# Spreading projections and softmax halves evenly over the slots of two attentions in a fused four-layer kernel

## The chip, the cores and the metric

The kernel runs as one program on one core of one Trainium2 chip. The core has five instruction streams that run beside each other: TensorE (PE in the profile; its weight loads are the row PEld), VectorE (DVE), ScalarE (ACT), GpSimd (POOL), and SyncE (SP), which in this kernel mostly issues transfers. Each stream executes strictly in its own order and waits on semaphores for the others. The metric is device time in microseconds (us) of one execution. Before the change the median of three runs was 3443.88 us (3443.7 to 3446.11).

## The reference, cut to what matters

Four layers are applied in turn to `x` of shape (8, 256, 512), all in fp32: an attention over features (layer 0), an RWKV block with a sequential scan (layer 1), a transformer decoder layer (layer 2) and a bilinear block with batch norm (layer 3). The change lies in the two attentions of layer 2, a self attention and a cross attention with the same arithmetic, eight batches each:

```python
def attention(q, k, v, mask):                      # 16 heads of 32, 256 queries, 256 keys
    scores = einsum('bhqd,bhkd->bhqk', q, k) / sqrt(HD)
    scores = scores * mask - 10000.0 * (1.0 - mask)
    probs = softmax(scores, axis=-1)
    return einsum('bhqk,bhkd->bhqd', probs, v)

ln_out = layernorm(hidden_states, ln1_s, ln1_b)
q, k, v = split(ln_out @ w_qkv + b_qkv, 3)
x = hidden_states + merge_heads(attention(...)) @ w_ao + b_ao       # then the same with w_q, w_kv, w_co,
                                                                    # keys and values from encoder_states
```

## The kernel before

The class `Middle` computes layer 1 and the two attentions. Its method `loop` has two parts. The first is the scan of layer 1, 64 steps ("slots" 0 to 63). The second is the attention part, again 64 slots, numbered on from `A0 = 64`. One *run* is one attention of one batch: runs 0 to 7 (`a_`) are the self attentions, 8 to 15 (`c_`) the cross attentions. A run has four slots (`CT = 4`), one for each group of four heads (`ct`); a slot has two halves `h2` of two heads each.

For each slot these functions exist (line numbers of the kernel before):

- `scores` (L1119): 8 products of PE, into four PSUM banks, one for each head.
- `masked` (L1131, L1134), a half: DVE multiplies the scores by the mask, adds the mask's offset, writes them to SBUF as `pe` and takes the maximum.
- `exps` (L1143), a half: ACT exponentiates in place and sums.
- `divided` (L1151, L1153), a half: DVE takes the reciprocal of the sums, POOL multiplies `pe` by it.
- `turn` (L1163, L1167, L1169), a half: DVE transposes 32x32 blocks of `pe` into `dt`, SP writes `dt` to a DRAM tile in one transfer, and four gathers from DRAM bring it back as `pt`, with keys on the partitions.
- `values` (L1182, L1186): 8 products of PE of `pt` with the values, then ACT takes the result out of PSUM as `cx`.

Everything else of a run is put as *fillers* at a position relative to the run's first slot, a table of positions that `fill.until` works off: the fetch of the batch (`at_fetch`), its layer norm (`at_norm`, `at_normed`, `at_norm_T`), encoder states and mask (`at_inputs`), halves of the projections (`at_q`, `at_k` by feature pairs at L817; `at_v`, `at_out` by row halves at L881), the residual (`at_residual`, L1079, L1081, L1087) and the store (`at_store`, L1093). A second table of the same positions says when the weights of the four projections are needed and until when, and from it the weight loads are placed.

Three things set the order on the engines. PE runs in exactly the order in which the code calls it (a manual schedule). Instructions wrapped in `pin` keep the program's order on their engine. All the rest on DVE, ACT and POOL, and SP's transfers, are placed by a scheduler between these.

In the loop before, the scores and masks stand two slots ahead of the block transposes, and the exponentials and divisions one slot ahead. Within a slot `n` the order is: exponentials of `n+1`, both transposes of `n`, scores of `n+2`, then in turn for both halves the masks of `n+2` and the divisions of `n+1`, then fillers up to position `n+0.5`, the values of `n-1`, and the rest of the fillers. In each run the fillers put projection halves into its slots unevenly: the positions modulo four give one half (`q`) in the first slot, four (two of `k`, two of `out`) in the second, one (`v`) in the third and two (`q`, `v`) in the fourth. PSUM has eight banks of one tag (`mm`), handed out in turn to scores, projections, transposed norms and values. `pt` has two buffers for each half, `pe` six.

Fillers of the last batches of layer 1 (the channel mix, at positions up to `A0 + 24`) still run beside the first runs of the attention part, and the first runs' own norm and projections run beside the last slots of the scan.

Of the kernel before, what the change touches and what calls it, by code (L numbers as in the profile page):

```python
# [17 lines left out]
B, S, D = 8, 256, 512  # L18
# [603 lines left out]
class Middle:  # L622
# [62 lines left out]
    def plan(self):  # L685
        g, cp, wpool = self.g, self.cp, self.wpool
        nc, I = g.nc, g.I
# [25 lines left out]
        def mm(name):  # L713
            return ps.tile([P, 2, S], F32, tag="mm", name=name, bufs=bufs[0])
# [180 lines left out]
        def spread(b, ct, hf):  # L895

            v_ = t_["v", b]
            vb = vbs[b, ct, hf] = ps.tile([P, NG, 2, S], F32, tag="vb", name="vb", bufs=1)
            for j in range(2):
                for n in range(NG):  # L900
                    r = slice(32 * n, 32 * n + 32)
                    nc.tensor.matmul(  # L902
                        vb[:, n, j, 1:S], lhsT=esel[r, 2 * hf + j, :], rhs=v_[r, ct, 0 : S - 1],
                        start=True, stop=True,
                    )
# [99 lines left out]
        pin = lambda ins: self.tc.keep_in_program_order(ins)  # L1005
# [89 lines left out]
        def at_load(W, src, col):  # L1095
            t_[W, 0] = rows_of(g.weight(wpool, I[src], col, W))
# [17 lines left out]
        def scores(i, ct):  # L1114
            sps = t_["sp", i, ct] = [mm("sp") for _ in range(NH)]
            for qt in range(ST):
                for h in range(NH):
                    r = slice(h * HD, (h + 1) * HD)
                    nc.tensor.matmul(  # L1119
                        sps[h][:, qt, :], lhsT=t_["aq", i][r, ct, qt * P : (qt + 1) * P],  # L1120
                        rhs=t_["ak", i][r, ct, :], start=True, stop=True,
                    )

        def masked(i, ct, h2):


            pe = t_["pe", i, ct, h2] = wk.tile([P, 2 * ST, S], F32, tag="a", name="pe", bufs=6)
            nmax = t_["nmax", i, ct, h2] = sm.tile([P, 2 * ST], F32, tag="nmax", name="nmax", bufs=4)
            for h in range(2):
                sp = t_["sp", i, ct][2 * h2 + h]  # L1130
                pin(nc.vector.scalar_tensor_tensor(sp, sp, 1.0 / HD ** 0.5, t_["mk", i], ALU.mult, ALU.mult))  # L1131
                for qt in range(ST):
                    r = ST * h + qt
                    pin(nc.vector.tensor_tensor_reduce(  # L1134
                        pe[:, r, :], sp[:, qt, :], t_["mb", i][:, qt, :], -1.0, 3.0e38, ALU.add, ALU.min,
                        nmax[:, r : r + 1],
                    ))

        def exps(i, ct, h2):
            pe, nmax = t_["pe", i, ct, h2], t_.pop(("nmax", i, ct, h2))  # L1140
            ssum = t_["ssum", i, ct, h2] = sm.tile([P, 2 * ST], F32, tag="ssum", name="ssum", bufs=4)
            for r in range(2 * ST):
                nc.scalar.activation(  # L1143
                    pe[:, r, :], pe[:, r, :], AF.Exp, bias=nmax[:, r : r + 1], scale=-1.0,
                    accum_out=ssum[:, r : r + 1],
                )

        def divided(i, ct, h2):
            pe = t_["pe", i, ct, h2]
            rinv = sm.tile([P, 2 * ST], F32, tag="rinv", name="rinv", bufs=4)  # L1150
            pin(nc.vector.reciprocal(rinv, t_.pop(("ssum", i, ct, h2))))  # L1151
            for r in range(2 * ST):
                pin(nc.gpsimd.tensor_scalar(  # L1153
                    pe[:, r, :], pe[:, r, :], rinv[:, r : r + 1], 1.0, ALU.mult, ALU.mult
                ))

        def turn(i, ct, h2):


            pe = t_.pop(("pe", i, ct, h2))  # L1160
            dt = wk.tile([P, 4, S], F32, tag="xn", name="dt", bufs=6)
            pt = t_["pt", i, ct, h2] = wk.tile([P, 4, S], F32, tag=("r", "w4")[h2], name="pt")
            pin(nc.vector.transpose(  # L1163
                dt.rearrange("p c (x q) -> p x c q", q=32), pe.rearrange("p x (k c q) -> p (x k) c q", k=ST, c=4)
            ))
            to = g.dram([4, 32, 4, S], f"pt{i}_{ct}_{h2}")
            nc.sync.dma_start(out=to.rearrange("r k c f -> (r k) c f"), in_=dt)  # L1167
            for c in range(4):
                nc.sync.dma_start(out=pt[32 * c : 32 * c + 32], in_=to[:, :, c].rearrange("r k f -> k r f"))  # L1169
# [48 lines left out]
        fill = self.fill = Filler()  # L1218
# [4 lines left out]
        A0 = 8 * B  # L1223
        for i in range(len(runs)):
            for at, fn, *args in (
                (-7.1, at_fetch), (-5.95, at_inputs), (-6.6, at_norm), (-5.9, at_normed), (-5.3, at_norm_T),
                (-4.8, at_q, 0), (-3.8, at_q, 1), (-2.8, at_k, 0), (-2.3, at_k, 1), (-1.3, at_v, 0), (-0.8, at_v, 1),
                (3.9, at_residual), (5.2, at_out, 0), (5.6, at_out, 1), (6.3, at_store),
            ):
                fill.put(A0 + CT * i + at, lambda i=i, fn=fn, args=args: fn(i, *args))  # L1230
        runs.append(("m_", 0))
# [14 lines left out]
        for pre, i, q, kv, o in (("a_", 0, "w_qkv", "w_qkv", "w_ao"), ("c_", B, "w_q", "w_kv", "w_co")):  # L1246
            c = D if q == kv else 0
            for W, lo, hi, src, col in (
                ("wq", -4.8, -3.8, q, 0), ("wk", -2.8, -2.3, kv, c), ("wv", -1.3, -0.8, kv, c + D), ("wo", 5.2, 5.6, o, 0)
            ):  # L1250
                lo, hi = A0 + CT * i + lo, A0 + CT * (i + B - 1) + hi
                spans.append((lo, hi, lambda W=pre + W, src=src, col=col: at_load(W, src, col)))
# [3 lines left out]
        for lo, hi, fn in spans:  # L1256
            free.sort()
            at = free.pop(0)
# [4 lines left out]
        def loop(psums):  # L1263
            every = [(b, ct, hf) for b in range(B) for ct in range(CT) for hf in range(2)]
            bufs[0] = 3
            fill.until(-0.001)
            spread(*every[0])
            for n, at in enumerate(every):
                states(*at)
                fill.until(n + 0.95)  # L1270
                if n:
                    gather(*every[n - 1])
                fill.until(n + 0.99)
                if n + 1 < len(every):
                    spread(*every[n + 1])
            gather(*every[-1])

            psums.close()
            self.ps = psums.enter_context(self.tc.tile_pool(name="atp", bufs=8, space=PSUM))
            bufs[0] = 8  # L1280
            every = [(i, ct) for i in range(2 * B) for ct in range(CT)]
            for at in every[:2]:
                scores(*at)
                masked(*at, 0)
                masked(*at, 1)
            for h2 in range(2):
                exps(*every[0], h2)
                divided(*every[0], h2)
            fill.until(A0 + 0.5)
            for n, at in enumerate(every):  # L1290
                one, two = every[n + 1 : n + 2], every[n + 2 : n + 3]
                for nxt in one:
                    exps(*nxt, 0)
                    exps(*nxt, 1)
                turn(*at, 0)
                turn(*at, 1)
                for nxt in two:
                    scores(*nxt)
                for h2 in range(2):
                    for nxt in two:  # L1300
                        masked(*nxt, h2)
                    for nxt in one:
                        divided(*nxt, h2)
                fill.until(A0 + n + 0.5)
                if n:
                    values(*every[n - 1])
                fill.until(A0 + n + 0.99)
            values(*every[-1])
            fill.until(999)
            psums.close()  # L1310
            return t_["ln", 2 * B]
# [454 lines left out]
```

## Time and profile before

| what | value |
|---|---|
| median of 3 runs | 3443.88 us |
| the profiled execution | 3449.99 us, its span 3448.2 us |
| attention part in it | from the first scores, 2170.66 us, to the first product of the next stage, 2949.84 us |
| PE busy over the span | 3211.6 us (93%) |
| DVE, ACT, POOL busy | 2409.5 us (70%), 1604.9 us (47%), 1667.2 us (48%) |
| transfers by SP's queue | 523.60 MB, 48.4% of the 16 engines' span |

A group of instructions is shown as line, engine, operation, written and read tiles, count, then busy time and mean duration, then idle time before it and who ended that. In a timeline the first column is the start in us from the span's start, the second the duration, the last brackets the idle time of the engine before it and what released it. SPq rows are the issues of transfers on SP. A table by windows gives, for each stretch, busy time of PE, weight loads, DVE, ACT and POOL with instruction counts in brackets, then the granted clock of PE (1.00 is full), the busy share of the DMA engines and GB/s.

### The profile page before, as it was taken

Reading aid. Unit: us, or ns where it says so; the run is one execution under the profiler, and the core shown is the slowest. Engines: PE = TensorE matmul, PEld = TensorE weight load, DVE = VectorE, ACT = ScalarE, POOL = GpSimd, SP = SyncE. Lnnn points to the kernel's source line nnn. Section 1 sums busy time; section 2 is a strip of 40 time slices with the busy share of each in tenths; the row PEclk is TensorE's granted clock in tenths of the full one; section 3 lists DMA queues with packets and bytes.
Section 4 is the critical chain, followed back from the end, with each engine's and each line's share of the span. In section 5 each row is a group of like instructions: output and inputs, shape, how many; then the busy total and the mean of one; then the engine's idle time right before and its main releaser. Section 6 shows DMA issues by size and latency. Waiting matters only on the chain. (4 is left out here: it accounts for less than half of the span.)

```text
span 3448.2 us, 68784 instructions
## 1 busy us (share of the span) xinstructions
PE 3211.6 (93%) x26496; PEld 2282.7 (66%) x26496; DVE 2409.5 (70%) x4175; ACT 1604.9 (47%) x4000; POOL 1667.2 (48%) x1776
## 2 busy tenths in 40 slices
PE   9999999999999988889999998899899996899999
PEld 6677777777777765555666665555555553689996
DVE  5667666666666663888788787767777776677771
ACT  4455555555555554233433334566656664323223
POOL 7533333333333222556566665344444443688872
PEclk9999999999999998989999999899999998899999
DMA  8666665665756533212232332578787877500002
GB/s 281 224 195 198 187 198 173 203 198 183 222 175 211 180 100 117 86 50 90 95 104 92 117 96 97 154 233 237 230 246 236 242 240 218 175 1 1 1 13 86
DMA packets 277366, 533.09 MB, mean 155 GB/s; under 512 B 25056, under 2 KB 153712, under 8 KB 272944
## 3 DMA queue, kind: packets, MB, share of 16 engines
q1 hardware_dynamic: 274144, 523.60, 48.4%
q8 instruction: 211, 3.46, 0.4%
q10 hardware_dynamic: 2224, 3.28, 0.3%
q0 software_dynamic: 672, 1.81, 0.2%
q14 instruction: 115, 0.94, 0.1%
HBM read 411.15 MB, written 117.44 MB: 153 GB/s over the span
## 5 line engine op out<-in xcount | busy, mean ns | idle before, releaser
L391 POOL TENSOR_SCALAR pe<-pe,rinv 128x512 f32<-128x512 f32 x256 | 177.8, 695 | 613.7 <-DVE rinv L390 611.1
L368 DVE TENSOR_REDUCE nmax<-sp 128x2 f32<-128x1024 f32 x256 | 309.0, 1217 | 182.6 <-PE sp L363 182.6
L933 POOL TENSOR_TENSOR rs<-a,r 128x1024 f32<-128x1024 f32 x128 | 303.3, 2386 | 242.4 <-DVE a L928 211.6
L1153 POOL TENSOR_SCALAR pe<-pe,rinv 128x256 f32<-128x256 f32 x512 | 236.3, 481 | 342.1 <-DVE rinv L1151 319.4
L377 ACT ACTIVATE pe<-sp,nmax 128x512 f32<-128x512 f32 x512 | 347.5, 683 | 11.2 <-ACT nmax L373 0.2
L1143 ACT ACTIVATE pe<-pe,nmax 128x256 f32<-128x256 f32 x512 | 255.9, 502 | 207.8 <-DVE nmax L1134 203.1
L403 DVE STREAM_TRANSPOSE pt<-pe 128x1024 f32<-128x1024 f32 x256 | 312.8, 1232 | 24.2 <-POOL pe L391 15.4
L432 PE MATMUL av<-pt,vr 32*64 32x256 f32 x8192 | 266.0, 390 | 41.2 <-issue 32.8
L928 DVE TENSOR_TENSOR_SCAN a<-w,vb 128x1024 f32<-128x1024 f32 x128 | 287.2, 2276 | 5.0
L432 PEld LDWEIGHTS av<-pt,vr 32*64 32x64 f32 x8192 | 209.3, 136 | 110.0 <-issue 65.8
L363 PE MATMUL sp<-k,q 64*64 64x512 f32 x2048 | 266.3, 612 | 5.6 <-ACT pe L377 5.6
L373 ACT ACTIVATE nmax<-nmax 128x2 f32<-128x2 f32 x256 | 52.0, 203 | 398.6 <-DVE nmax L368 398.5
L1163 DVE STREAM_TRANSPOSE dt<-pe 128x1024 f32<-128x1024 f32 x128 | 156.9, 1234 | 69.7 <-POOL pe L1153 68.6
L303 PEld LDWEIGHTS gp<-t,ws 128*128 128x128 f32 x1512 | 184.8, 192 | 30.7 <-ACT pe L396 11.4
L303 PE MATMUL gp<-t,ws 128*128 128x128 f32 x1512 | 202.1, 277 | 2.2 <-POOL ws L289 1.4
L396 ACT ACTIVATE pe<-pe,rinv 128x512 f32<-128x512 f32 x256 | 182.7, 730 | 41.2 <-DVE rinv L390 41.2
L924 DVE TENSOR_TENSOR vb<-vb,k 128x1020 f32<-128x1020 f32 x128 | 157.2, 1228 | 4.4
L1182 PE MATMUL cp<-pt,av 128*32 128x256 f32 x1024 | 93.4, 422 | 69.3 <-DMA pt<-pt 57.1
L1445 ACT ACTIVATE h<-h,pvec 128x256 f32<-128x256 f32 x124 | 55.9, 502 | 199.9 <-DVE h L1414 162.7
L902 PE MATMUL vb<-v,mconstc 32*128 32x255 f32 x1024 | 98.8, 441 | 52.6 <-DVE a L928 52.6
L390 DVE RECIPROCAL rinv<-ssum 128x2 f32<-128x2 f32 x256 | 41.2, 161 | 147.3 <-ACT pe L377 147.3
L455 PEld LDWEIGHTS op<-av_sb,wo 128*128 128x128 f32 x512 | 93.3, 192 | 55.9 <-issue 27.5
(310 smaller groups left out, 7618.8 us busy)
## 6 DMA issues: line engine op xcount, KB each, us to landing
pt<-dt SPq DMA_DIRECT2D x128, 512.0 KB, 4.3
pt<-pt SPq DMA_DIRECT2D x512, 128.0 KB, 3.9
ws<-sqk SPq DMA_DIRECT2D x110, 512.0 KB, 4.9
wqk<-in_wqk_dram SPq DMA_DIRECT2D x70, 512.0 KB, 5.5
vr<-v SPq DMA_DIRECT2D x128, 256.0 KB, 4.6
ws<-sv SPq DMA_DIRECT2D x56, 512.0 KB, 4.8
wv<-in_wv_dram SPq DMA_DIRECT2D x36, 512.0 KB, 5.3
v<-vT SPq DMA_DIRECT2D x64, 256.0 KB, 2.6
```

The costliest lines, as they stand in the source:

```text
L303: nc.tensor.matmul(out[:, hf * P : (hf + 1) * P], lhsT=w[n](hf, k), rhs=a[n](hf, k), start=k == 0, stop=k == ST - 1,)
L363: nc.tensor.matmul(sp[a * 64 : (a + 1) * 64, h, :], lhsT=qs[b, 2 * un + a][r, ic], rhs=ks[b, 2 * un + a][r, :], start=True, stop=True,)
L368: nc.vector.tensor_reduce(nmax, sp, AX.X, ALU.max, negate=True)
L377: nc.scalar.activation(pe[:, h, :], sp[:, h, :], AF.Exp, bias=nmax[:, h : h + 1], scale=1.0 / DH ** 0.5, accum_out=ssum[:, h : h + 1],)
L391: nc.gpsimd.tensor_scalar(pe[:, 0, :], pe[:, 0, :], rinv[:, 0:1], 1.0, ALU.mult, ALU.mult)
L396: nc.scalar.mul(pe[:, 1, :], pe[:, 1, :], rinv[:, 1:2])
L403: nc.vector.transpose(pts[b, un][:, it], pe)
L432: nc.tensor.matmul(av[r][h * DH : (h + 1) * DH], lhsT=vr[rows_, kb, h * DH : (h + 1) * DH], rhs=pt[rows_, :, h, 32 * kb : 32 * kb + 32], s ...
L928: nc.vector.tensor_tensor_scan(a.rearrange("p n l -> p (n l)"), w4.rearrange("p n l -> p (n l)"), vb[:, 4 * n2 : 4 * n2 + 4, :].rearrange( ...
L933: nc.gpsimd.tensor_tensor(rs, a, rb, ALU.mult)
L1143: nc.scalar.activation(pe[:, r, :], pe[:, r, :], AF.Exp, bias=nmax[:, r : r + 1], scale=-1.0, accum_out=ssum[:, r : r + 1],)
L1153: pin(nc.gpsimd.tensor_scalar(pe[:, r, :], pe[:, r, :], rinv[:, r : r + 1], 1.0, ALU.mult, ALU.mult))
```

## The change

Three edits. First, the loop of the attention part is written anew as a stream of half slots: in slot `n` the scores of `n+1` come first; then twice, for each half `k` of slot `n+1`: masks of `k`, exponentials of `k`, division of `k-1`, transpose of `k-2`; then all the slot's fillers; then the values of `n-1`, last in the slot. Scores and masks are now one slot ahead instead of two, and there is one slot of prologue instead of two. Second, the fillers' positions change so that each slot of a run has two projection halves: both of `v` (with the transposed norm of the next run between them) in the first, `q` and `out` in the second, `k` and `out` in the third, `q` and `k` in the fourth; fetch, norm, inputs and weight loads move with them, and they stand one to two slots later. Third, the exponentials are pinned in program order on ACT.

```diff
@@ exps
             for r in range(2 * ST):
-                nc.scalar.activation(
+                pin(nc.scalar.activation(
                     pe[:, r, :], pe[:, r, :], AF.Exp, bias=nmax[:, r : r + 1], scale=-1.0,
                     accum_out=ssum[:, r : r + 1],
-                )
+                ))
@@ plan: fillers of a run
-                (-7.1, at_fetch), (-5.95, at_inputs), (-6.6, at_norm), (-5.9, at_normed), (-5.3, at_norm_T),
-                (-4.8, at_q, 0), (-3.8, at_q, 1), (-2.8, at_k, 0), (-2.3, at_k, 1), (-1.3, at_v, 0), (-0.8, at_v, 1),
-                (3.9, at_residual), (5.2, at_out, 0), (5.6, at_out, 1), (6.3, at_store),
+                (-5.2, at_fetch), (-4.6, at_norm), (-4.1, at_normed), (-3.5, at_norm_T), (-3.1, at_inputs),
+                (-2.8, at_q, 0), (-1.8, at_k, 0), (-0.8, at_q, 1), (-0.3, at_k, 1), (0.2, at_v, 0), (0.7, at_v, 1),
+                (4.1, at_residual), (5.7, at_out, 0), (6.7, at_out, 1), (6.8, at_store),
@@ plan: use of the weights
-                ("wq", -4.8, -3.8, q, 0), ("wk", -2.8, -2.3, kv, c), ("wv", -1.3, -0.8, kv, c + D), ("wo", 5.2, 5.6, o, 0)
+                ("wq", -2.8, -0.8, q, 0), ("wk", -1.8, -0.3, kv, c), ("wv", 0.2, 0.7, kv, c + D), ("wo", 5.7, 6.7, o, 0)
@@ loop
-            for at in every[:2]:
-                scores(*at)
-                masked(*at, 0)
-                masked(*at, 1)
-            for h2 in range(2):
-                exps(*every[0], h2)
-                divided(*every[0], h2)
-            fill.until(A0 + 0.5)
-            for n, at in enumerate(every):
-                one, two = every[n + 1 : n + 2], every[n + 2 : n + 3]
-                for nxt in one:
-                    exps(*nxt, 0)
-                    exps(*nxt, 1)
-                turn(*at, 0)
-                turn(*at, 1)
-                for nxt in two:
-                    scores(*nxt)
-                for h2 in range(2):
-                    for nxt in two:
-                        masked(*nxt, h2)
-                    for nxt in one:
-                        divided(*nxt, h2)
-                fill.until(A0 + n + 0.5)
-                if n:
+            stream = [(i, ct, h2) for i, ct in every for h2 in range(2)]
+            for n in range(-1, len(every)):
+                if n + 1 < len(every):
+                    scores(*every[n + 1])
+                for k in (2 * n + 2, 2 * n + 3):
+                    if k < len(stream):
+                        masked(*stream[k])
+                        exps(*stream[k])
+                    if 0 < k <= len(stream):
+                        divided(*stream[k - 1])
+                    if 1 < k:
+                        turn(*stream[k - 2])
+                fill.until(A0 + n + 0.95)
+                if n > 0:
                     values(*every[n - 1])
                 fill.until(A0 + n + 0.99)
             values(*every[-1])
```

## The prediction

> **What bounds the kernel now.** I read first the table by windows over the attention part, cut at the first scores, at the point where the channel mix has mostly run out, at the last scores but two, and at the next stage's first product.
>
> ```profile
> 2171.00:2411.80 240.80, 229.81 (x1215) 138.57 (x1207) 175.52 (x516) 146.67 (x448) 97.95 (x175) 0.97 0.75 219
> 2411.80:2879.80 468.00, 423.13 (x2361) 252.02 (x2361) 356.85 (x1050) 280.11 (x874) 194.83 (x374) 0.93 0.79 238
> 2879.80:2949.80 70.00, 41.84 (x193) 17.16 (x192) 31.43 (x87) 19.96 (x65) 21.54 (x40) 0.73 0.81 240
> ```
>
> In the first stretch PE (first figure after the length) is busy 95%, and from 2200 on 98%: nothing but less work would shorten it. In the second, 468 us, PE is busy 90% at a clock of 0.93, DVE 76%: neither is full. The third, the drain, has PE busy 60% at 0.73.
>
> Next the timeline of PE over one run of the second stretch, for its work and its holes.
>
> ```profile
> 2646.63 1.15 PE L1119 MATMUL sp<-ak,aq 32*128 32x256 f32 x16
> 2647.71 1.07 PE L1182 MATMUL cp<-pt,av 128*32 128x256 f32 x16
> 2648.71 3.70 PE L881 MATMUL projs<-c_wv,enc 128*128 128x512 f32 x8
> 2652.24 1.04 PE L83 MATMUL ln_tp<-ident,axn 128*128 128x128 f32 x8
> ...
> 2673.95 3.70 PE L881 MATMUL projs<-c_wo,cx 128*128 128x512 f32 x8
> 2677.49 3.62 PE L817 MATMUL proj<-enc,c_wk 128*128 128x256 f32 x16
> 2681.03 1.07 PE L1182 MATMUL cp<-pt,av 128*32 128x256 f32 x16
> 2682.03 3.70 PE L881 MATMUL projs<-c_wo,cx 128*128 128x512 f32 x8
> 2685.57 3.62 PE L817 MATMUL proj<-enc,c_wk 128*128 128x256 f32 x16
> 2689.12 1.15 PE L1119 MATMUL sp<-ak,aq 32*128 32x256 f32 x16
> ...
> 2712.48 0.63 PE L1182 MATMUL cp<-pt,av 128*32 128x256 f32 x4 [2.28 <-DVE nmax L1134]
> 2714.61 1.92 PE L1182 MATMUL cp<-pt,av 128*32 128x256 f32 x12 [1.51 <-DMA pt<-pt]
> 2716.47 2.09 PE L1119 MATMUL sp<-ak,aq 32*128 32x256 f32 x16
> ```
>
> From start to start: scores 1.08, values 1.00, a projection half 3.54, transposed norm 0.97. A run's PE work at full clock is 4x1.08 + 4x1.00 + 8x3.54 + 0.97 = 37.6 us. But scores of the same place in the run stand at 2411.78 and 2869.39, ten runs apart: 45.8 us a run. Two things show where 8 us go. Between the scores at 2672.88 and 2689.12 lie four projection halves, 16.2 us, in which DVE has only 8 to 9 us of work; in the lighter slots PE in turn waits, 2.28 and 1.51 us here. And after these waits PE is slow: the same scores take 2.09 instead of 1.15 us.
>
> Then the timeline of SP, for the way from a transpose to the values, and of DVE, for half a slot.
>
> ```profile
> 2890.10 0.32 SPq L1167 DMA_DIRECT2D pt<-dt  x1
> 2890.53 4.34 SPq L1169 DMA_DIRECT2D pt<-pt  x8
> ```
>
> ```profile
> 2703.41 0.68 DVE L1131 SCALAR_TENSOR_TENSOR sp<-sp,mk 128x512 f32<-128x512 f32 x1
> 2706.24 0.17 DVE L1151 RECIPROCAL rinv<-ssum 128x4 f32<-128x4 f32 x1
> 2708.39 1.25 DVE L1163 STREAM_TRANSPOSE dt<-pe 128x1024 f32<-128x1024 f32 x1 [0.85 <-POOL pe L1153]
> ```
>
> On SP a single write of `dt` is followed by eight gathers, the last four of which need it. Half a slot of masks takes DVE 2.83 us (2703.41 to 2706.24), the reciprocal 0.08, a transpose 1.17 net. The transpose waits for POOL, 44.5 us in the second stretch.
>
> **The change part by part.**
>
> *Projections, two to a slot.* No instruction is added or removed: 64 slots keep their 8+8 products, 16 masks and maxima, eight exponentials, 2 transposes, 10 transfers. PE's slots become 10.1 us (two `v` and the norm) and three times 9.2 (1.08 + 2x3.54 + 1.00). DVE's slot is 2x(2.83 + 0.08 + 1.17) = 8.2, plus a run's two residual adds, two statistics, two aggregations and one small product at 0.67, 0.67, 0.17 and 0.16: 3.2 a run, so 9.0 a slot. ACT: eight times 0.69, 0.47 for `cx`, about 1 of drains: 7.0, and once a run 3.1 of tables and layer norm. All are under 10. The 16.2 us hole of DVE is gone.
>
> *Half slots in turn.* A division of half k-1 is issued after the masks of k, its transpose after the masks of k+1, 4.1 us later; POOL needs 1.85 for four of its multiplications. So the transpose's waits for POOL go, except where the residual's two adds (2.5 us) fall between. An exponential's half ends 4.0 us after its masks began, and the reciprocal comes at 7.0: 3 us spare, which covers table loads and drains. These cost nothing while that spare lasts; beyond it DVE waits. Pinning fixes the same order and costs nothing by itself.
>
> *Values at the slot's end.* This adds the new wait. On PE behind the values stand the scores of the next slot but one half-step of DVE away: if `pt` is late, PE, then DVE, then ACT and POOL wait. The loop goes over two slots: scores start to first mask 1.2 us (2170.66 to 2171.85), DVE's slot 9.0, issue 0.1, write landed, four gathers issued, landed, values 1.0. For a write issued alone: the eight gathers at 2890.53 took 4.34 us against 3.66 for eight without a wait, so the fifth left about 2.9 us after its write at 2890.10. Ahead of it on SP now stand the write's own issue, mostly one other transfer (0.5 to 1.0) and the four gathers of the first half (4x0.46): 2.8 to 3.3. I take 3.1. To the last gather's issue 3x0.46 = 1.4, landing 4.0 (median of 168). Together 1.2 + 9.0 + 0.1 + 3.1 + 1.4 + 4.0 + 1.0 = 19.8 us for two slots. The DMA engines are 0.79 busy at 45.8 us a run; at 42 that is 0.86. The part of a landing above its minimum (4.0 less 2.6) I stretch by half for this, 0.7 on each of the two transfers: 21.2 us. So a run lasts 42.4 us, above PE's 37.6. The bounds: 38.5 if the loop hides (PE's work and 0.9 of entries), and 50.4 if the way stays as in the old pair of halves, where it took 14.0 us from the transpose's end at 2700.58 to the values at 2714.61 (loop 25.2). I take the value near the lower one because that old row holds a second write, a blocked encoder load ahead of it and eight gathers behind, and the single write at 2890.10 is the new pattern. Gain: 10 runs x (45.8 - 42.4) = 34 us.
>
> *Clock.* At 2.28 + 1.51 us of waits the scores that follow run at half speed. The forecast leaves about 1.2 us of wait in a slot, in one piece, which I expect to stay warm: the run from 2646.63 to 2689.12 had waits up to 1.97 and ran warm, in 42.5 us.
>
> The Trainium skill, "TensorE: Matmul & The Clock Gate", section "Part 1: The HAM clock gate", says that PE falls to half clock after an idle window of about 3.4 us and needs as long a busy one to recover. It speaks against a wait in every slot; the row above agrees that it is the clock, but falls after two waits of 2.28 and 1.51 with work between. By that rule alone nothing is lost at my 1.2 us, and by the row's pattern a run in which that happens costs 3 us (45.7 against 42.5 for the warm run).
>
> *Start.* Before the first scores PE's order loses both `v` of run 0 and one `q` and a norm of run 1: 3x3.54 + 1 = 11.6 us that move from the scan, where DVE is the bound, into a stretch where PE is. Against that, PE idled 7.9 us in 2170 to 2200 in the two-slot prologue, now filled, and the scan's end has DVE waits of 5.7 and 3.8 behind such fillers. Between +11.6 and -9; I take 0, the sum's middle.
>
> *Drain.* From scores of slot 60 (2869.39) to 2949.84 it took 80.5 us, since SP held three writes in order (gathers 4 us late), and the late transposes stood behind a pinned residual add that waited 7.46 us for PE. Now: slots with `q`+`k`, `v`+`v` and one `out`, 3x10.6; then 9.0 of DVE, 3.5 for the last division and transpose, 10 to `pt`, 1.9 of values and 8 of `out` at the low clock: 64. Gain 16 (8 to 18).
>
> *SP, POOL, weights.* Encoder loads stood ahead of writes and waited for `v` (34.7 us in 240); now they come after the slot's second write, when `v` is done. Their cover is gone if PE lags DVE by over 1 us. POOL's other work (norm, mask offset, residual: 1.5, 0.6, 2.5 us a run) fits in its idle half. The next stage's first weights are issued among the last gathers instead of after them (eight at 2934.59); PE did not wait for them, I count nothing. PSUM: the next scores need banks whose masks ended 1 to 2 us earlier: nothing, below 2 us of lag.
>
> **The sum.** 3449.99 - 34 - 16 - 0 = 3400.0 for an execution like the profiled one, which is 6.1 above the median: 3394.
>
> **The rivals.**
> 1. *PE becomes the bound.* The loop stays under 19 us. For it: writes alone land at 2.6 at best, the first stretch shows PE at 98%. Against: DMA busy 0.86. Runs of 38.5: -73, drain -18: 3353.
> 2. *No gain in the runs.* The way from transpose to `pt` is 12.5 us, loop 22.9, run 45.8; the drain alone remains: 3428.
> 3. *Slower.* The same way keeps the old 14.0 us: landings of 7.4 (the longest seen) at the busier queue. For it: scores stood two slots ahead before and hid this; now they don't. Run 50.4, +46 over ten; drain -8: 3482. It decides against the old kernel from a way of 13.3 us on, where 10 runs cost the drain's 16.
>
> **How the numbers follow.** Forecast 0.52 (own range 3372 to 3420), rival 1 0.18, rival 2 0.10, rival 3 0.20. A measurement of this kernel tells about 0.2% (7 us) from no change. Rival 2 gives the chance of no change (half of its spread) 0.05; faster 0.75, slower 0.20. Range: 3350 to 3452 leaves out rival 3.
>
> **What would show it.** Right: in the middle stretch scores 10 to 11 us apart, clock 0.97 or more, waits of values for `pt` of 1 to 2 us in most slots, no waits of transposes for POOL, drain near 64 us. Wrong: values waiting over 3 us with scores at 2.1 us (rival 3), PE without holes (rival 1), reciprocals waiting for ACT (the spare of 3 us used up).

## The result, and the profile after

The changed kernel takes 3456.23 us (median of 5 runs, 3455.25 to 3463.92) against 3443.88 for the kernel before (5 runs): a ratio of 1.0046, 95% interval 1.0028 to 1.0064. It is slower by 0.46%, where 3394 us was forecast. The profiled execution took 3462.03 us, its span 3460.3.

The table by windows of the changed kernel, cut as before at the first scores, at the scores of slots 20 and 60, and at the next stage's first product (busy time of PE, weight loads, DVE, ACT and POOL, then clock, DMA share, GB/s):

```profile
2168.00:2410.90 242.90, 230.86 (x1236) 139.59 (x1236) 176.40 (x518) 151.89 (x454) 103.41 (x183) 0.98 0.76 222
2410.90:2885.50 474.60, 412.22 (x2322) 247.34 (x2320) 346.74 (x1032) 278.08 (x860) 191.81 (x370) 0.94 0.80 231
2885.50:2961.30 75.80, 50.23 (x252) 24.56 (x251) 37.81 (x104) 24.90 (x81) 19.40 (x39) 0.80 0.85 243
```

The start is neutral. The middle stretch holds ten runs (scores of slot 20 to scores of slot 60): 474.6 us, where 457.6 stood before and 424 was forecast. The drain, the third line, is 75.3 from start to start, before 80.5, forecast 64. The profiled execution missed the forecast of 3400.0 for one execution by 62.0 us; this splits into -0.9 at the start, 50.6 in the ten runs, 11.3 in the drain and 1.0 behind it.

The timeline of PE of the changed kernel, first a stall, then a run from scores to scores without a long one:

```profile
2590.77 0.62 PE L1182 MATMUL cp<-pt,av 128*32 128x256 f32 x4
2600.37 1.92 PE L1182 MATMUL cp<-pt,av 128*32 128x256 f32 x12 [8.98 <-DMA pt<-pt]
2602.22 2.09 PE L1119 MATMUL sp<-ak,aq 32*128 32x256 f32 x16
...
2694.25 1.15 PE L1119 MATMUL sp<-ak,aq 32*128 32x256 f32 x16
...
2715.82 1.15 PE L1119 MATMUL sp<-ak,aq 32*128 32x256 f32 x16
...
2736.88 1.37 PE L1119 MATMUL sp<-ak,aq 32*128 32x256 f32 x16
```

From 2694.25 to 2736.88 a run takes 42.6 us, the forecast's length; two of the ten take 43.0 or less, the others 45 to 58. In the first rows the values wait 8.98 us for `pt`; the scores behind them run at half speed (2.09). A second such wait of 9.62 us stands at 2793.44. On SP the reason for the first of them reads as follows:

```profile
2583.39 1.74 SPq L1169 DMA_DIRECT2D pt<-pt  x4
2585.98 6.09 SPq L1167 DMA_DIRECT2D pt<-dt  x2
2594.56 0.38 SPq L1021 DMA_DIRECT2D mk<-in_mask_b_dram  x1
2595.06 3.98 SPq L1169 DMA_DIRECT2D pt<-pt  x8
```

The row of two writes, 6.09 us from the first's start to the second's end, holds the second half of one slot and the first half of the next; the four gathers that the values wait for are issued behind both and behind a mask's load, as the first four of the eight at 2595.06.

Last, what DVE and PE waited for in the ten runs (us in total, times, longest), in the kernel before and then in the changed one:

```profile
DVE dt L1163 <- POOL pe L1153: 44.5, 34, 6.4
DVE sp L1131 <- PE sp L1119: 17.2, 12, 1.9
PE cp L1182 <- DMA pt<-pt: 28.2, 16, 3.5
```

```profile
DVE sp L1131 <- PE sp L1119: 85.5, 29, 7.7
DVE away L1032 <- ACT ln_rstd L61: 16.9, 10, 3.4
DVE dt L1163 <- POOL pe L1153: 11.5, 3, 4.1
DVE ln_stats L58 <- DMA axi<-xa: 7.7, 3, 4.3
PE cp L1182 <- DMA pt<-pt: 56.0, 27, 9.6
```

The transposes' waits for POOL fell as forecast, from 44.5 to 11.5 us. In their place DVE waits 85.5 us for scores (before 17.2) and PE 56.0 for `pt` (before 28.2): DVE has become dependent on PE, which stands at the values. The statistics of the layer norm now wait for the fetch, which they did not in the kernel before.

### The profile page after: what moved, and what is told of

Read it like the earlier page. It is cut to its first block, busy times and chain, and to the rows that moved or that the text cites. A ratio compares the mean times of both kernels' runs of the same rounds, so it can differ in the third digit from the quotient of the medians.

```text
span 3460.3 us, 68721 instructions
## 1 busy us (share of the span) xinstructions
PE 3202.3 (93%) x26496; PEld 2286.0 (66%) x26496; DVE 2406.2 (70%) x4175; ACT 1607.7 (46%) x4000; POOL 1663.7 (48%) x1776
## 5 line engine op out<-in xcount | busy, mean ns | idle before, releaser
L377 ACT ACTIVATE pe<-sp,nmax 128x512 f32<-128x512 f32 x512 | 347.0, 683 | 11.2
L1182 PE MATMUL cp<-pt,av 128*32 128x256 f32 x1024 | 103.4, 424 | 94.4 <-DMA pt<-pt 83.0
L1182 PEld LDWEIGHTS cp<-pt,av 128*32 128x32 f32 x1024 | 36.8, 115 | 167.2 <-issue 104.9
```

Of the source, the lines that this page charges most:

```text
L377: nc.scalar.activation(pe[:, h, :], sp[:, h, :], AF.Exp, bias=nmax[:, h : h + 1], scale=1.0 / DH ** 0.5, accum_out=ssum[:, h : h + 1],)
```

## The experiments

All times are medians beside runs of the kernel before on the same chip; "a run" is a tenth of the ten runs from slot 20 to 60, measured at DVE's first mask product of a slot, in one profile; clock and DMA share are those of that stretch, where they were read. The profiled execution can lie off the median: that of x5_oldplaces took 14 us more, x1_order's 8 more, z5_closed_stats's 7 less. "Tied" means that SP's transfers stand in the order of x1_order, described below; x4_all and all runs whose names begin with x7, y or z1 to z5 are tied too.

| label | loop | places of projections | ratio to before, 95% | us | a run | clock, DMA |
|---|---|---|---|---|---|---|
| before | old | old | 1 | 3439 to 3444 | 46.0 | 0.93, 0.79 |
| after | new | even | 1.0046 (1.0028 to 1.0064) | 3456.2 | 47.5 | 0.94, 0.80 |
| x5_oldplaces | new | old | 1.0141 (1.0123 to 1.0159) | 3491.0 | 49.8 | 0.92, 0.76 |
| x6_evenold | old, tied | even, one slot earlier | 0.9920 (0.9905 to 0.9935) | 3416.5 | 43.4 | 0.96, 0.85 |
| x1_order | new, tied | even | 1.0043 (1.0026 to 1.0060) | 3454.2 | 46.7 | 0.94, 0.81 |
| x2_mask | new | even | 1.0064 (1.0041 to 1.0086) | 3464.1 | 47.1 | |
| x3_norm | new | even | 0.9996 (0.9984 to 1.0008) | 3440.7 | 44.7 | 0.98, 0.84 |
| x4_all | new | even | 0.9990 (0.9977 to 1.0004) | 3438.2 | 45.2 | |
| z5_closed_stats | new | even | 0.9980 (0.9969 to 0.9991) | 3434.6 | 43.9 | 0.99, 0.85 |
| z6_closed_wgwg | new | even | 1.0310 (1.0293 to 1.0327) | 3548.7 | 52.6 | 0.91, 0.66 |
| x7_first_oldplaces | new, scores first | old | 1.0018 (1.0006 to 1.0031) | 3450.8 | 46.6 | |
| y1_first | new, scores first | even | 0.9882 (0.9863 to 0.9902) | 3400.9 | 42.3 | 0.98, 0.89 |
| z2_stats | new, scores first | even | 0.9778 (0.9762 to 0.9795) | 3365.0 | 39.4 | 0.99, 0.94 |
| y5_first_mask | new, scores first | even | 0.9930 (0.9915 to 0.9945) | 3419.1 | 44.5 | 0.98, 0.84 |
| z1_stats_mask | new, scores first | even | 0.9897 (0.9882 to 0.9912) | 3405.9 | 42.9 | 0.95, 0.86 |
| z3_mask_later | new, scores first | even | 0.9806 (0.9781 to 0.9832) | 3373.7 | 39.8 | 1.00, 0.93 |
| z4_evenold_stats | old, tied | even, one slot earlier | 0.9903 (0.9886 to 0.9920) | 3406.0 | 42.0 | 0.98, 0.87 |

### The two parts of the change, each alone

x5_oldplaces keeps the new loop and puts the two tables of positions back. x6_evenold keeps the loop of before, has the projections evenly placed, each one slot earlier than in the changed kernel, and ties SP's order besides:

```diff
-                (-7.1, at_fetch), (-5.95, at_inputs), (-6.6, at_norm), (-5.9, at_normed), (-5.3, at_norm_T),
-                (-4.8, at_q, 0), (-3.8, at_q, 1), (-2.8, at_k, 0), (-2.3, at_k, 1), (-1.3, at_v, 0), (-0.8, at_v, 1),
-                (3.9, at_residual), (5.2, at_out, 0), (5.6, at_out, 1), (6.3, at_store),
+                (-6.2, at_fetch), (-5.6, at_norm), (-5.1, at_normed), (-4.5, at_norm_T), (-5.95, at_inputs),
+                (-3.8, at_q, 0), (-2.8, at_k, 0), (-1.8, at_q, 1), (-1.3, at_k, 1), (-0.8, at_v, 0), (-0.3, at_v, 1),
+                (4.1, at_residual), (5.2, at_out, 0), (6.2, at_out, 1), (6.3, at_store),
```

> One part of the change alone: the new stream by half slots, with all fetches, projections and stores at their old places (two projections in some slots, none in others). Theory 'loop' with late inputs: the inputs are early as before, but slots with three products (3.5 us each) make TensorE late for the scores; 3435 to 3450. Rival 'the stream gains and the moved places lose': 3410 to 3425. Rival 'the stream loses': 3460 or above.

> The other part of the change alone: the old loop (both halves of a slot behind each other, scores two slots ahead) with the projections one to a half slot as in the changed kernel, each one slot earlier than there, since the old loop asks for the scores a slot earlier; SP's four transfers of a slot in the order of x1_order. Theory 'loop': the old loop is held by VectorE's waits for POOL (44.0 us in ten runs) and by output projections that come late behind the others (24.6 us); the second goes with even places, the first stays: 3415 to 3435. Rival 'even places gain nothing on their own': 3438 to 3450.

Even places in the old loop gain 26 us, as the loop theory had it; the tied order stands in that number too, and what it is worth in the old loop was not tried alone. The new loop alone loses 48 us by the ratio and 52 by the medians, which only the third theory allowed. Before and after lie 12 to 16 us apart: some 26 gained, some 40 lost. So the change's two parts pull in opposite directions, and the forecast gave the gain to both. What DVE waits for in the ten runs, of x6_evenold and then of x5_oldplaces:

```profile
DVE dt L1163 <- POOL pe L1153: 36.6, 42, 1.6
DVE sp L1131 <- PE sp L1119: 24.4, 16, 3.4
```

```profile
DVE sp L1131 <- PE sp L1119: 94.7, 32, 6.5
DVE dt L1163 <- POOL pe L1153: 13.0, 3, 8.5
```

The half-slot order does take away most of the waits for POOL, and each time brings more waits for scores.

### Late inputs: queue order, mask, layer norm

x1_order ties the transfers of a slot on SP to the order write 0, write 1, gathers 0, gathers 1 (each tied behind the one before it by `follow`, an edge without a wait):

```diff
+            follow(nc.sync.dma_start(out=to.rearrange("r k c f -> (r k) c f"), in_=dt))
+            for h in range(2 * h2):
+                to, pt = t_.pop(("to", h)), t_["pt", i, ct, h]
+                for c in range(4):
+                    follow(nc.sync.dma_start(out=pt[32 * c : 32 * c + 32], in_=to[:, :, c].rearrange("r k f -> k r f")))
```

x2_mask moves the mask's load from -3.1 to -5.95 and its offset `mb` to -3.9; x3_norm moves `(-5.2, at_fetch), (-4.6, at_norm), (-4.1, at_normed)` to -7.1, -6.6, -5.9; x4_all is all three.

> The changed kernel with one thing more: on SP each slot's four transfers stand as write 0, write 1, gathers 0, gathers 1, so that no gathers stand behind the next slot's write; in the changed kernel they do at three slots, (0,0), (8,1) and (12,1), counted as run and slot. Theory 'queue order': the two waits of the values for pt, 8.98 us at 2600.4 and 9.62 us at 2793.4, stand just there and go, with about 2 us each of half-speed products behind them; 16 to 20 us less than the changed kernel's 3456, so 3436 to 3440. Rival 'the way is too long': the values wait for the way wherever it stands, the two waits spread over the next slots, and the time stays within 4 us of 3456.

> The changed kernel with the mask's load back at its old place (-5.95) and its offset on POOL at -3.9, the context's load left at -3.1. Theory: POOL's 37 us of waits for the mask (8 times) go, and SP's order at (8,1) and (12,1) comes back of itself (one slot of the three, (0,0), is left); 16 to 20 us for the order and 2 to 8 us for the divisions that no longer stand behind a waiting offset: 3430 to 3439. Rival 'only the order counts': as x1_order. Rival 'the way is too long': within 4 us of 3456.

> The changed kernel with the next run's fetch, statistics and normalization back at -7.1, -6.6 and -5.9 (its transposes stay at -3.5); the mask's load stays late. SP's order at (8,1) and (12,1) comes back here too. Theory: 16 to 20 us for the order, and the waits of the statistics (10 us) and of the transposes behind the normalization go, some 3 to 10 us with the cold products behind them: 3426 to 3437. Rival 'only the order counts': as x1_order. Rival 'the way is too long': within 4 us of 3456.

> The order of x1_order, the mask of x2_mask and the fetch of x3_norm together. Theory 'the stream is as short as forecast and the loss is late transfers': all ten runs come to the 42.6 to 43.5 us that three of the ten show in the changed kernel (mean there 47.5), so 40 to 49 us less, 3407 to 3416. Rival 'the way is too long': runs stay at 45 us and more, 3431 or above.

x1_order refuted my theory: the two long stalls are gone, and the time is that of the changed kernel (1.0043 against 1.0046). The waits spread out, as the rival had it; eight of the ten runs take 45.5 to 47.7. Something else held the stretch, and the stalls had been inside it. x2_mask gained nothing either; in its profile the statistics wait 26.4 us for the fetch (7.7 in the changed kernel), which stands against what POOL saved. x3_norm gained 13 to 17 us, and six of its seven cross-attention runs among the ten take 42.7 to 43.5. So the late fetch and layer norm counted, the two stalls by themselves did not. But the gain is not a shorter wait of the statistics: in x3_norm's profile they wait 22.4 us for the fetch, in the changed kernel 10.3. What fell is DVE's wait for scores (85.5 to 56.0) and the transposes' wait for POOL (11.5 to 0.3). Which of the three moved operations did that was not tried. x4_all added nothing to x3_norm. None came near the 3410 of "the loss is late transfers".

### Opening the loop

In the changed kernel PE computes a slot's values, then the next scores. y1_first is x1_order with this:

```diff
                 if n + 1 < len(every):
                     scores(*every[n + 1])
+                if n > 1:
+                    values(*every[n - 2])
...
                 fill.until(A0 + n + 0.95)
-                if n > 0:
-                    values(*every[n - 1])
                 fill.until(A0 + n + 0.99)
+            values(*every[-2])
```

> x1_order with the scores of the next slot put ahead of the values in TensorE's order (values of a slot at the start of the second step behind it, not at the end of the next): the first 'scalar_tensor_tensor' of a slot no longer stands behind a product that waits for pt. Theory 'loop': the two-slot loop write, gather, values, scores, mask has no slack in the changed kernel, so that every late thing on VectorE comes back through it; VectorE's waits for scores (24.1 us in the four runs from slot 32 of x1_order) go, and the runs fall from 46.7 to 41.5 to 43 us, which leaves VectorE full: 3405 to 3420. Rival 'late inputs': VectorE waits as long, only for the statistics' input and POOL instead: 3448 or above. Rival 'transfers': pt lands later still, the values wait longer and TensorE is late for the scores after them: 3448 or above, with longer waits of cp for pt.

> y1_first and the early fetch, statistics and normalization of x3_norm. Theory 'loop': the loop is open and the inputs are early; VectorE is the bound with 41.4 us of instructions and gaps in a run: ten runs of 41.5 to 42.5, 3398 to 3412. Rival 'late inputs alone': as x3_norm, 3437 to 3444.

> y1_first with the early fetch and the early mask of x4_all, and the small product 'away' of VectorE left out (POOL subtracts the mean and multiplies by the deviation's inverse in its one instruction, the same value but for rounding), so that VectorE no longer waits for ScalarE's logarithm and exponential (11.0 us in the four runs from slot 32 of x4_all). Theory 'loop': 3392 to 3406. Rival 'late inputs alone': 3430 to 3438.

> x5_oldplaces with the scores ahead of the values as in y1_first, and SP's order as there: old places of all projections, open loop. Theory 'loop': most of the 47 us that the new stream lost with the old places was the loop's lack of slack against slots with three products; with the loop open 3405 to 3435. Rival 'TensorE's uneven slots hold VectorE by themselves': 3460 or above.

y1_first takes 3400.9 us, 53 less than x1_order, by moving eight products behind eight others. The waits of x1_order and then of y1_first:

```profile
DVE sp L1131 <- PE sp L1119: 72.7, 29, 6.6
PE cp L1190 <- DMA pt<-pt: 43.9, 32, 4.8
```

```profile
DVE sp L1131 <- PE sp L1119: 29.4, 21, 3.1
PE cp L1190 <- DMA pt<-pt: 17.6, 16, 3.1
```

That is the loop theory, with a time 4 us below its range, and neither rival. x7_first_oldplaces shows it from the other side: 40 us less than x5_oldplaces (whose queue order it also ties). It stays 50 above y1_first and so misses its own forecast: even places are worth 47 to 50 us with the open loop, 33 to 35 with the closed one, 26 with the old (there with the tied order in the number). y2_first_norm, with the early fetch, was expected to be better than y1_first and came out some 6 us worse, within its own forecast and with intervals that overlap, so that no gain is all that can be said: in its profile the statistics wait 19.1 us for the fetch (0.8 in y1_first). y3_first_all (ratio 0.9906, 0.9891 to 0.9921) has the same wait, 14.9 us; y2_first_norm's ratio is 0.9900 (0.9884 to 0.9916).

My sentence in these expectations that DVE is full at 41 us of instructions a run was wrong: I had added up rows of the timeline that overlap. By the table of windows DVE's busy time is 35 us a run, and z2_stats below runs at 39.4.

### Who stands at the head of a queue

Two runs that I expected to gain by an earlier mask lost instead:

> y1_first with the mask's load at -5.95 and its offset at -3.9 as in x2_mask. In y1_first POOL still waits 37.6 us for the mask in four goes and VectorE 23.6 us for POOL. Theory 'VectorE is full': y1_first's runs are 42.3 and VectorE's instructions with their gaps 41.0, so at most 1.3 a run is to be had, 8 to 13 us: 3388 to 3393. Rival 'another wait takes its place' (scores, statistics): within 5 us of 3401.

> y5_first_mask without VectorE's product 'away' (POOL subtracts the mean and scales in its one instruction). Theory 'VectorE is full': ten products of 0.65 us and 17 us of waits for ScalarE go from VectorE; 3380 to 3390. Rival 'POOL takes the wait': POOL stands 32 us for ScalarE as in y3_first_all and holds the divisions behind it; 3393 to 3408.

y5_first_mask took 3419.1 us, 18 more than y1_first, and y6_first_mask_naw, which drops the product `away` besides, 3454.0 (1.0033, 1.0021 to 1.0046). In y5_first_mask POOL no longer holds the transposes, but two new heads of queues do, one on DVE, one on SP:

```profile
DVE ln_stats L58 <- DMA axi<-xa: 35.3, 7, 6.0
SPq L1019 <- DVE sp L1142: 36.7, 6, 6.2
```

The first: the mask's load took the fetch's place in SP's order, the fetch went a slot later (in y1_first it is issued at 2613.73, 8.7 us ahead of slot 40's scores; in y5_first_mask at 2631.76, 9.1 us behind them), and the statistics, which stand in DVE's order ahead of the masks pinned behind them, wait for it. The second: the early mask's load waits for the last reader of its buffer, which in the new order is one slot later than in the old, and gathers stand behind it. Two runs tell these apart. z1_stats_mask takes the first away and keeps the second; z2_stats takes the early mask away as well:

```diff
-        nc.vector.bn_stats(stats[:, st, :], xb[:, st, :])
-        nc.vector.bn_aggr(mv[:, st, :], stats[:, st, :])
+        pin(nc.vector.bn_stats(stats[:, st, :], xb[:, st, :]))
+        pin(nc.vector.bn_aggr(mv[:, st, :], stats[:, st, :]))
...
-            nc.vector.scalar_tensor_tensor(away, mv[:, :, 0], -1.0, rstd, ALU.mult, ALU.mult)
+            pin(nc.vector.scalar_tensor_tensor(away, mv[:, :, 0], -1.0, rstd, ALU.mult, ALU.mult))
...
-                (-5.2, at_fetch), (-4.6, at_norm), (-4.1, at_normed)
+                (-7.1, at_fetch), (-5.6, at_norm), (-4.9, at_normed)
```

> y5_first_mask with the fetch at -7.1, the statistics at -5.6 and the product 'away' at -4.9, each in a step of its own and held in that place in VectorE's order, so that their inputs have a slot (10 us) and more to come. Theory 'head of VectorE': the 41.3 us of waits of the statistics for the fetch and most of the 26.9 us of 'away' for ScalarE go; VectorE is full at 41.0 a run: runs of 41 to 42.3, 3386 to 3400. Rival 'the early mask itself costs' (its load among the gathers, its offset on POOL): 3412 to 3422, as y5_first_mask.

> The same without the early mask: y1_first with fetch, statistics and 'away' at -7.1, -5.6 and -4.9, held in place. Theory 'head of VectorE': 17.2 us of waits for ScalarE go, the 23.6 us behind POOL's mask offset stay: 3390 to 3402. Rival 'the fetch among the gathers costs', as in y2_first_norm: 3405 to 3412.

> z1_stats_mask with the mask's load about a slot later, at -4.9, and held behind the gathers that stand before it. Theory 'head of SP': the 40.4 us of SP's waits for the mask's buffer go, gathers are punctual, and the time is z2_stats's: 3362 to 3375. Rival 'the early offset on POOL or the load's traffic costs': 3395 to 3410.

z1_stats_mask came to 3405.9 us, between its theory and its rival; z2_stats to 3365.0, below both; z3_mask_later to 3373.7, as its theory had it. In z1_stats_mask the wait of the statistics is gone and that of SP is not; its SP timeline:

```profile
2641.80 3.82 SPq L1178 DMA_DIRECT2D pt<-dt  x2
2652.43 0.38 SPq L1019 DMA_DIRECT2D mk<-in_mask_b_dram  x1
2652.91 3.73 SPq L1182 DMA_DIRECT2D pt<-pt  x8
```

From the end of the first row at 2645.62 SP stands 6.8 us for the mask's buffer, then issues eight gathers whose writes it had issued 7 us and more before. z3_mask_later moves that one load about a slot later and holds it behind the gathers, with no other edit, and is 32 us faster. So the early mask cost by its place at the head of SP, not by its traffic. What the early mask cost in x4_all was not separated.

z2_stats is the fastest kernel of the study, 2.2% under the kernel before. Its stretch of ten runs, and PE in one run:

```profile
2404.50:2798.90 394.40, 386.29 (x2315) 237.41 (x2309) 349.58 (x1031) 274.25 (x861) 190.29 (x367) 0.99 0.94 277
```

```profile
2640.97 1.15 PE L1119 MATMUL sp<-ak,aq 32*128 32x256 f32 x16
2642.05 1.64 PE L1190 MATMUL cp<-pt,av 128*32 128x256 f32 x16
2643.61 3.72 PE L817 MATMUL proj<-ln,c_wq 128*128 128x256 f32 x16
2647.17 3.62 PE L817 MATMUL proj<-enc,c_wk 128*128 128x256 f32 x16
2650.72 1.15 PE L1119 MATMUL sp<-ak,aq 32*128 32x256 f32 x16
...
2679.23 1.15 PE L1119 MATMUL sp<-ak,aq 32*128 32x256 f32 x16
```

Scores lead, values follow, no brackets: PE is busy 98% at a clock of 0.99, and a run takes 38.3 us here, near the 37.6 of PE's work.

### The loop by itself

With punctual statistics, z5_closed_stats has the changed kernel's own loop again, and z4_evenold_stats the old one.

> x6_evenold with the fetch, the statistics and 'away' at -8.1, -6.6 and -5.9, each in a step of its own and held in place. Theory 'the stream gains with an open loop': the old loop keeps VectorE's waits for POOL (36.3 us in ten runs of x6_evenold) and loses the 17.5 us for ScalarE: 3395 to 3408. Rival 'only late inputs counted': 3362 to 3375, as z2_stats.

> z2_stats with the values back at the slot's end, ahead of the next scores: the changed kernel's own loop, with punctual statistics and SP's order kept. Theory 'loop': two slots take the 21.2 us that the prediction worked out, 42.4 a run against z2_stats's 39.4, and some ten us more where other work of VectorE falls into the loop: 3395 to 3415. Rival 'late statistics alone made the loss': 3365 to 3375.

z5_closed_stats is 3434.6 us: 20 less than x1_order (fetch, statistics and `away` earlier and held in place) and 70 more than z2_stats (the loop). The loop theory gave 30 to 50 over z2_stats, so the time lies outside its range, and far above the rival's. By the two profiled executions it is 55, of which 44 lie in the ten runs. What the edit took out of DVE's waits of x1_order, and what z5_closed_stats still waits for:

```profile
DVE ln_stats L58 <- DMA axi<-xa: 13.3, 4, 4.6
DVE away L1032 <- ACT ln_rstd L61: 13.0, 10, 3.4
```

```profile
DVE sp L1131 <- PE sp L1119: 69.3, 30, 7.0
PE cp L1190 <- DMA pt<-pt: 36.8, 35, 3.5
```

The same edit is worth 36 us with the open loop (y1_first to z2_stats) and 6 to 10 with the old one, each place one slot earlier (x6_evenold to z4_evenold_stats). So late statistics cost least in the old loop, but they cost in the open one too: the closed loop is not their only way into the time. z4_evenold_stats is 3406.0, as forecast. So with everything punctual the order is: open half-slot loop, old loop, closed half-slot loop. The loop of z5_closed_stats over two slots, from scores to scores:

```profile
2772.75 1.15 PE L1119 MATMUL sp<-ak,aq 32*128 32x256 f32 x16
...
2793.82 1.06 PE L1190 MATMUL cp<-pt,av 128*32 128x256 f32 x12 [1.36 <-DMA pt<-pt]
2794.81 1.15 PE L1119 MATMUL sp<-ak,aq 32*128 32x256 f32 x16
```

```profile
2773.91 0.70 DVE L1131 SCALAR_TENSOR_TENSOR sp<-sp,mk 128x512 f32<-128x512 f32 x1 [2.08 <-PE sp L1119]
...
2780.90 1.22 DVE L1163 STREAM_TRANSPOSE dt<-pe 128x1024 f32<-128x1024 f32 x1
```

1.2 us to the mask, 8.2 of DVE, 11.7 from the transpose's end to the values, 1.0 of values: 22.1. Over the pairs of slots from slot 20 to 60, from DVE's first mask product to that of the next slot but one, the median is 21.4 to 21.5 us, in the changed kernel 23.6 to 23.8, in z2_stats 19.2 to 19.4.

z6_closed_wgwg was to shorten the way within that loop, with the gathers of a half directly behind its write:

```diff
-            for h in range(2 * h2):
+            for h in (h2,):
```

> z5_closed_stats with SP's order in a slot changed from write 0, write 1, gathers 0, gathers 1 to write 0, gathers 0, write 1, gathers 1. The second half's gathers then have no gathers of the first half between their write and themselves: four issues of 0.46 us, 1.5 to 1.8 us less on the way. Theory 'the way is in the loop': two slots take as much less, a run 3 to 3.6 us less than the 43.9 of z5_closed_stats, 40.3 to 41: 3395 to 3408. Rival 'not the way': 3430 to 3440.

It took 3548.7 us, outside both forecasts: I had the sign wrong. SP's waits in its ten runs, and its timeline (a write, then gathers, in turn):

```profile
SPq L1171 <- DMA pt<-dt: 195.2, 61, 5.1
```

```profile
2755.36 1.81 SPq L1171 DMA_DIRECT2D pt<-pt  x4
2757.28 0.36 SPq L1167 DMA_DIRECT2D pt<-dt  x1
2762.13 2.01 SPq L1171 DMA_DIRECT2D pt<-pt  x4
2764.24 0.38 SPq L1167 DMA_DIRECT2D pt<-dt  x1
2764.71 0.40 SPq L1019 DMA_DIRECT2D enc<-in_ctxT_dram  x1
2768.34 1.74 SPq L1171 DMA_DIRECT2D pt<-pt  x4
```

Each write is followed by 3.2 to 4.5 us in which SP does nothing but wait until it has landed; a half slot takes SP 6 to 7 us, a slot 13.2, and a run 52.6. SP had become the bound (its 105.0 us of waits for a transpose in z5_closed_stats are gone), and the next write stood behind the waiting gathers: the way grew instead of shrinking (waits for `pt` of 90.9 us against 36.8). That a longer way lengthens the runs fits the loop; that a shorter one would shorten them is not shown by this run. The Trainium skill, "DMA: Bandwidth & Descriptors", section "Two DMAs through the same engine are not ordered", asks that the issuing engine wait on the first transfer's semaphore before the dependent one. This kernel does so; what z6_closed_wgwg adds is the price when nothing stands between the two.

## Why the prediction was wrong, step by step

- *Projections, two to a slot.* Right in kind. In the old loop, with SP's order tied, they gain 26 us of the 34 forecast for the runs (x6_evenold).
- *Half slots in turn, POOL's waits gone.* Right: 44.5 to 11.5 us. ACT was no limit; the ten runs show no reciprocal waiting for ACT. Exponentials without their pin were not tried.
- *Values at the slot's end, 21.2 us for two slots.* The mechanism was right and the size nearly so: 21.5 at the median with punctual inputs, 43.9 a run against 42.4. This step's 1.5 us make 15 of the 50.6 us. In the pair shown the way took 11.7 us where the forecast had 10.0, and DVE's slot 8.2 where it had 9.0.
- *What failed is the step "SP, POOL, weights", and with it DVE's slot of 9.0 us.* Norm, mask offset and residual were costed at nothing because POOL is half idle; the later fetch has no term at all; and the 9.0 us count the statistics and the small product `away` by their durations, without a wait. The engines are half idle, but they stand in order. A statistic that waits for its input stands ahead of a mask, a mask's offset ahead of the divisions, a load ahead of gathers. In the changed kernel the statistics wait 10.3 us in the ten runs (before: none) and `away` 16.9 (before: 19.5, so this wait is old). Late inputs and SP's order make the other 36 of the 50.6 us: SP's order 8 of them (x1_order, 466.8 us against 474.6), fetch, statistics and `away` 28 (z5_closed_stats, 438.7). That split is from one profiled execution of each. By the medians of the whole kernel the order gave 2 us at most and the rest 20, so that z5_closed_stats is still 40 us above the forecast of 3394. Its profiled execution is 28 us above 3400.0: 15 in the ten runs, 16 in the drain, 4 gained at the start. That the waits come back two slots later through the values is argued from the order, not isolated; nor were the waits of POOL for mask and residual in the closed loop.
- *Clock.* 0.97 or more was forecast, 0.94 came, with the late inputs. Without them it is 0.99 although the values wait 36.8 us in 35 pieces (z5_closed_stats): waits of about 1 us in most slots do stay warm, as the forecast had it.
- *Start.* 0, as forecast. But the 0 was the middle between +11.6 and -9, and which of the two came about was not looked into: the hit is luck.
- *Drain.* 75.3 instead of 64: the values waited 9.03 us at 2936.76 and 6.03 at 2946.90 for `pt`. SP issued one load of the next stage's weights between the last two writes and their gathers, for which "I count nothing" stood; that was not tested alone. With even places the closed loop needs 74 to 80 in every run but z6_closed_wgwg (89), and z2_stats, with the loop open, 74.6 (from 2797.00 to 2871.61). So the 64 were too few whatever the inputs did; the cause stays open.
- *Rival 3* (slower, the way keeps 14 us) had the sign, not the cause. The landings are as forecast (medians 3.3 us for a write, 4.4 for a gather, where the rival needed 7.4); the excess was waiting in the order of the queues. *Rival 1* (PE becomes the bound) describes z2_stats, where the loop was opened.
- *A slip in the rivals' sums.* By the forecast's own terms the loop is the way and 11.2 us (1.2 + 9.0 + 1.0), as in rival 3, where 14.0 gives 25.2. Rival 2's 12.5 then gives 23.7, not 22.9; its 22.9, and the 13.3 from which the change loses, come out only with 8.2 for DVE's slot. With 9.0, a run of 45.8 needs a way of 11.7, and the change loses from 12.5 on. The margin between the forecast and a loss was 0.8 us smaller than stated.

## What to carry to other kernels

Before costing a new place for a load or a small operation at nothing because its engine is idle, ask what stands behind it in that engine's order, and how many stages ahead the consumer runs: with one slot of lookahead in place of two, waits of 1 to 5 us for inputs cost more here (20 us against 6 to 10 by the same edit). Where a product that waits for a round trip stands ahead of one that feeds the next stage, swap them: here that alone was worth 53 us. And try the parts of a change apart: here one gained and the other lost more.

## What was not expected of the hardware

- SP, as a stream of issues, is a resource: with write and dependent gathers back to back it was the bound at 13.2 us a slot, while the DMA engines were 0.66 busy (z6_closed_wgwg); with another write between them and nothing else changed the share was 0.85 and a slot 11.0 us (z5_closed_stats), and with the loop open the same transfers ran at 0.94 and 277 GB/s (z2_stats).
- On POOL, subtracting one per-partition operand and multiplying by another took 2067 ns on 128x512 (y6_first_mask_naw), multiplying and adding 762 (y1_first), on the same tile:

```profile
L1043 POOL TENSOR_SCALAR axn<-axi,ln_mv,ln_rstd x34: 2057/2067/2076, 2070.1 to 2893.8; 128x512 f32<-128x512 f32 x34
```

```profile
L1034 POOL TENSOR_SCALAR axn<-axi,ln_rstd,away x34: 762/762/769, 2071.6 to 2841.6; 128x512 f32<-128x512 f32 x34
```

  y6_first_mask_naw is 35 us slower than y5_first_mask. This instruction and POOL's wait of 62.0 us for ScalarE ahead of it, with the divisions behind, are the likely reasons; how much each makes was not tried.
- More traffic did not make transfers slower in proportion: the median landing of a gather is 3.9 us before (DMA share 0.79) and 4.3 in z2_stats (0.94).
